# A transformer block in float32: the first tile's normalization ahead of the second tile's statistics, and the first batch's VectorE and GpSimd work in another order

## The chip, the cores and the metric

The kernel runs on one core of one Trainium2 chip. The metric is the device time of one execution in microseconds (us), lower is better. The profile shows one such execution. The engines are TensorE (PE, with its weight loads as PEld), VectorE (DVE), ScalarE (ACT), GpSimd (POOL) and SyncE (SP, which here only issues DMAs).

## The reference, cut to what matters

The input x has 8 batches of 1024 rows of 256 values, in float32. Each batch is normalized, goes through linear attention with l2-normed q and k, and through a two-layer network, and both are added to x:

```python
xn = _layernorm(x, axis=-1)
# attention, 16 heads of 16
qkv = (xn @ qkv_w + qkv_b).reshape(b, n, 3, H, D)
q, k, v = ...
q = q / max(norm(q), EPS);  k = k / max(norm(k), EPS)
kv = einsum('bhnd,bhne->bhde', k, v)
attn = einsum('bhnd,bhde->bhne', q, kv)  # then (b, n, c)
attn = attn @ proj_w + proj_b
# network, 256 -> 1024 -> 256
ffn = relu(xn @ W1 + b1) @ W2 + b2
return x + attn + ffn
```

## The kernel before, in words

A batch is 8 tiles of 128 rows (`NT`), two halves of four tiles (`HT`). The network's first layer, the projection to q and k (from batch 1 on), the product of k and xn and the second layer are computed by Strassen's scheme in Winograd's form: seven block products in place of eight, with sums of blocks formed ahead of the products (`sums_of_x`, `sums_of_h`, `sums_of_w2`, `g_sums`, on GpSimd) and sums of results formed from PSUM (`add`, on VectorE).

The order of all work is written out by hand: each engine executes its instructions in the order in which the program issues them. Buffers in PSUM come from a pool of seven banks (`bank`); an eighth tile takes the bank that the program's order freed first, and waits for its last reader.

*Head.* x of batch 0 is loaded in small pieces, the first two of one tile each. For tiles 0 and 1, `norm_stats` forms mean and variance (VectorE) and the root (ScalarE), `norm_scale` the reciprocal, `norm_apply` xn (VectorE, L276), and `turn_tile` transposes xn on TensorE (tpx, L899) and copies it out of PSUM on ScalarE (L900). `project(0)` then runs q and k of all eight tiles (pq, L331), with the normalization of tiles 2 to 7 in between, adds the bias on VectorE (L337), squares on ScalarE (L341) and sums the squares (L342).

*First layer, `hidden(b)`.* Twelve steps work on four blocks i: `first(i)` runs the products pha, phc and phd, with u1 copied by ScalarE and u2 and u3 formed by VectorE; `fifth(i)` runs phe; `last(i)` finishes three of the products; the relus (L650) are ScalarE's. The steps are, by number: 0 first(0), 1 fifth(0), 2 first(1), 3 last(0), 4 fifth(1), 5 first(2), 6 last(1), 7 fifth(2), 8 first(3), 9 last(2), 10 fifth(3), 11 last(3). After a step come `sums_of_x` of the next batch (steps 10 and 11), `sums_of_h` (0 after step 3, 1 after step 6, 2 and 3 after step 11), and the small steps that a table names: `first_steps` for batch 0, `later_steps` for the others.

*Small steps of batch 0.* `invert` turns the sums of squares into inverse norms: a maximum (L360, VectorE), a root (L361, ScalarE), a reciprocal (L362, VectorE). `scale` multiplies them into k and q (L474). `shift` adds one to a half of xn on ScalarE (L503), and `mix_g` multiplies k with xn (gp, L510) into gT. `fold_bias_of_v` folds the bias of v into its weights: a product of_rows (L493, TensorE), a (L495) and the sum onto the weights (L498), both VectorE. `mix_kv` (kvp, L604, then kvm on VectorE) reads these weights and gT; `mix_m` (mp, L621) reads kvm. The next batch's statistics and xn (L250 to L276) are formed; `turn_x`, called four times, transposes xn in blocks on VectorE (L298), each time followed by four DMAs on SP's queue (L300) that bring the parts to their partitions. After the twelve steps q of batch 0 is transposed on TensorE (tpq, L286), and `project_by_sums(1)` begins with pqa (L406).

After that, `second(b)` runs the second layer and the last product with q, and stores; all further batches follow the same pattern with `later_steps`.

Of the kernel before, what the change touches and what calls it, by code (L numbers as in the profile page):

```python
# [10 lines left out]
AF = mybir.ActivationFunctionType  # L11
# [5 lines left out]
def kernel(  # L17
# [34 lines left out]
    nc = tc.nc  # L52
# [5 lines left out]
    NT = N // P  # L58
    HT = NT // 2
# [5 lines left out]
    R = P // S  # L65
# [3 lines left out]
    L2_EPS = 1e-12  # L69
# [15 lines left out]
    def squares_v(v, b, n, j):  # L85


        return v[b].rearrange("(n s r t) (j c) -> n j s r t c", n=2, s=S, r=R, j=R)[n, j]

    def bank(shape, name):  # L90

        return psum.tile(shape, F32, tag="bank", name=name)
# [15 lines left out]
    def load_squares(b, halves=(0, 1)):  # L108
        xqs[b] = one.tile([P, 2, R, HT, CJ], F32, tag="xq", name=f"xq_{b}")
        for n in halves:  # L110
            for j in range(R):
                nc.sync.dma_start(out=xqs[b][ts(j, S), n], in_=squares_v(x, b, n, j))
# [124 lines left out]
    def s3_of_x(b):  # L237

        a11, a12, a21, a22 = halves(xnTs[b])
        nc.gpsimd.tensor_tensor(a21, a11, a21, ALU.subtract)  # L240
# [3 lines left out]
    def norm_stats(b, tiles):  # L244

        xt, n = xs[b], len(tiles)
        st = work.tile([P, NT, 6], F32, tag="st", name=f"st_{b}_{tiles[0]}")[:, :n, :]
        mv = small.tile([P, NT, 2], F32, tag="mv", name=f"mv_{b}_{tiles[0]}")[:, :n, :]
        for i, t in enumerate(tiles):
            nc.vector.bn_stats(st[:, i, :], xt[:, t, :])  # L250
        for i in range(n):
            nc.vector.bn_aggr(mv[:, i, :], st[:, i, :])
        rstd = small.tile([P, NT], F32, tag="rstd", name=f"rstd_{b}_{tiles[0]}")[:, :n]
        nc.scalar.activation(rstd, mv[:, :, 1], AF.Sqrt, bias=eps_sb)
        for i, t in enumerate(tiles):
            stats[b, t] = i, mv, rstd

    def norm_scale(b, tiles, on_act):
        i, mv, rstd = stats[b, tiles[0]]
        nc.vector.reciprocal(rstd, rstd)  # L260
        if on_act:
            nmr = small.tile([P, NT], F32, tag="nmr", name=f"nmr_{b}_{i}")[:, : len(tiles)]
            nc.vector.scalar_tensor_tensor(nmr, mv[:, :, 0], -1.0, rstd, ALU.mult, ALU.mult)  # L263
            for t in tiles:
                stats[b, t] += (nmr,)

    def norm_apply(b, tiles):
        for t in tiles:
            xt, xn = xs[b][:, t, :], xns[b][:, t, :]
            i, mv, rstd, *nmr = stats.pop((b, t))  # L270
            if nmr:
                nc.scalar.activation(  # L272
                    xn, xt, AF.Identity, bias=nmr[0][:, i : i + 1], scale=rstd[:, i : i + 1]
                )
            else:
                nc.vector.tensor_scalar(  # L276
                    xn, xt, mv[:, i, 0:1], rstd[:, i : i + 1], ALU.subtract, ALU.mult
                )
# [28 lines left out]
    def turn_x(b):  # L307

        if b not in xnTs:
            xnTs[b] = big.tile([P, KC, NP, P, 2], F32, tag="xnT", name=f"xnT_{b}")  # L310
            turns["x", b] = turn(xnTs[b], xns[b], f"x_{b}")
        next(turns["x", b])

    def project(b, within={}, held_to=0, with_norms=True):


        xnT = xnTs[b]
        if b not in qks:
            qks[b] = one.tile([P, NT, 2 * C], F32, tag="qk", name=f"qk_{b}")
        qk = qks[b]  # L320
        late, held = [], []
        for h in range(2):
            ss = small.tile([P, HT, 2 * H], F32, tag="ssk" if h else "ssq", name=f"ss_{b}_{h}", bufs=1)
            all_ss[b, h] = ss
            for s in range(2):
                norms_of[b, h, s] = ss[:, :, ts(s, H)]
            for i in range(HT):
                t = h * HT + i
                pq = bank([P, 512], f"pq_{b}_{t}")
                for kc in range(KC):  # L330
                    nc.tensor.matmul(  # L331
                        pq, xnT[:, kc, t // 2, :, t % 2], wqkv_sb[:, kc, 0 : 2 * C],
                        start=(kc == 0), stop=(kc == KC - 1), skip_group_check=True,
                    )
                    if kc == 0:
                        within.get(t, lambda: None)()
                nc.vector.tensor_tensor(qk[:, t, :], pq, qkvb_sb[:, 0 : 2 * C], ALU.add)  # L337

                def square(t=t, ss=ss, i=i):
                    sq = work.tile([P, 2 * C], F32, tag="yt", name=f"sq_{b}_{t}")  # L340
                    nc.scalar.activation(sq, qk[:, t, :], AF.Square)  # L341
                    return lambda: nc.vector.tensor_reduce(  # L342
                        ss[:, i, :], sq.rearrange("p (g d) -> p g d", d=D), AX.X, ALU.add
                    )

                held.append(square)
                while held and t >= held_to:
                    late.append(held.pop(0)())
                    while len(late) > 1:
                        late.pop(0)()  # L350
                if i == HT - 1 and with_norms:
                    late.append(lambda h=h, ss=ss: norms(b, h, ss))
        while late:
            late.pop(0)()

    norms_of, all_ss = {}, {}

    def invert(ss):

        nc.vector.tensor_scalar_max(ss, ss, L2_EPS * L2_EPS)  # L360
        nc.scalar.activation(ss, ss, AF.Sqrt)  # L361
        nc.vector.reciprocal(ss, ss)  # L362

    def norms(b, h, ss):
        invert(ss)
        scale(nc.gpsimd, b, h, 1)

    wt = const.tile([P, 3, C], F32, tag="wt", name="wt")
    dbias = const.tile([P, C], F32, tag="dbias", name="dbias")
# [101 lines left out]
    def scale(eng, b, h, s):  # L471

        part = qks[b][:, ts(h, HT), ts(s, C)].rearrange("p t (g d) -> p t g d", d=D)
        eng.tensor_tensor(  # L474
            part, part,
            norms_of[b, h, s].unsqueeze(3).to_broadcast([P, HT, H, D]), ALU.mult,
        )

    def scale_q(b, h):
        scale(nc.gpsimd if b == 0 else nc.vector, b, h, 0)  # L480

    def turn_q(b):

# [5 lines left out]
    def fold_bias_of_v():  # L489

        wv = wqkv_sb[:, :, of_v]
        of_rows = bank([P, C], "of_rows")
        nc.tensor.matmul(of_rows, mean, wv[:, 0, :], start=True, stop=True)  # L493
        a = one.tile([P, C], F32, tag="ksum", name="a")
        nc.vector.scalar_tensor_tensor(  # L495
            a, qkvb_sb[:, of_v], 1.0 / P, of_rows, ALU.mult, ALU.subtract
        )
        nc.vector.tensor_tensor(wv, wv, a.unsqueeze(1).to_broadcast([P, KC, C]), ALU.add)  # L498

    def shift(b):  # L500

        part = xns[b][:, :, 0:P]
        nc.scalar.activation(part, part, AF.Identity, bias=ones)  # L503

    def mix_g(b):
        qk, xn = qks[b], xns[b]
        gp = ps_mix.tile([P, KC, C], F32, tag="mix", name=f"gp_{b}")
        for f in range(KC):
            for t in range(NT):
                nc.tensor.matmul(  # L510
                    gp[:, f, :], xn[:, t, ts(f, P)], qk[:, t, C : 2 * C],
                    start=(t == 0), stop=(t == NT - 1),
                )
        gT = one.tile([P, KC, C], F32, tag="gT", name=f"gT_{b}")
        nc.scalar.copy(gT, gp)
        mixes[b] = gT
# [205 lines left out]

    def first_steps(b):

        lo, hi = range(HT), range(HT, NT)
        return {
            0: [lambda: load_squares(b)] + [lambda h=h: norms(b, h, all_ss[b, h]) for h in range(2)],
            1: [
                lambda: norm_stats(b + 1, lo), lambda: scale_q(b, 0), lambda: scale_q(b, 1),
            ],  # L730
            2: [lambda: shift(b), lambda: norm_stats(b + 1, hi), lambda: norm_scale(b + 1, lo, True)],
            4: [
                lambda: norm_scale(b + 1, hi, False), lambda: norm_apply(b + 1, lo),
                lambda: norm_apply(b + 1, hi), fold_bias_of_v, lambda: mix_g(b),
            ] + [lambda: turn_x(b + 1)] * R,
            5: [lambda: shift(b + 1), sums_of_w2, lambda: g_sums(b + 1, 0)],
            6: [lambda: mix_kv(b)],
            10: [lambda: mix_m(b)],
            11: [lambda: load(b + 2)],
        }  # L740

# [159 lines left out]

    for t in range(2):
        norm_stats(0, (t,))
    for t in range(2):
        norm_scale(0, (t,), False)
        norm_apply(0, (t,))
        turn_tile(t)
# [16 lines left out]
    def tiles_4_to_7():  # L924
# [5 lines left out]
        sums_of_x(0, 0)  # L930
        sums_of_x(0, 1)

    project(0, {1: tiles_2_3, 3: tiles_4_to_7}, 3, False)
    s3_of_x(0)
    sums_of_wqk()
    load(1)
# [70 lines left out]
```

## Time and profile before

| what | value |
|---|---|
| three runs, median (lowest to highest) | 617.99 us (617.8 to 619.47) |
| the profiled execution's own time | 617.92 us |
| its span in the profile | 616.1 us |
| TensorE busy | 606.6 us (98%) |
| VectorE, GpSimd, ScalarE busy | 417.3, 423.6, 211.5 us |
| pqa, the first product of batch 1's projection, starts at | 59.43 us |
| poa of batch 0's second layer starts at | 71.5 us |

Times in the timeline count from the start of the span. A row has start, duration, engine, line, operation, output<-inputs and count; in square brackets stands how long the engine was idle before it, and what ended that. A row of the waits reads: engine, tile and line that waited, what it waited for, then total, times and longest in us. Rows of the timeline are merged where the same line follows itself on an engine; the row's duration is then that of the whole stretch.

### The profile page before, as it was taken

How to read it: one execution, taken by the hardware profiler on the slowest of the kernel's cores; microseconds unless marked ns; L12 is line 12 of the kernel's file. 1: busy time of each engine (PE TensorE's matmuls, PEld its weight loads, DVE VectorE, ACT ScalarE, POOL GpSimd, SP SyncE). 2: the span in 40 equal slices, each digit the busy share in tenths (PEclk: the TensorE clock that was granted, in tenths of full speed). 3: DMA queues.
4: the chain of work that ended last, by engine and by line, in shares of the span. 5: the costliest groups of instructions: out<-in, count | busy, mean ns of one | idle time of the engine just before them, and what ended most of it. 6: DMA issues, size and time to landing. Idle time of an engine off the chain costs nothing.

```text
span 616.1 us, 6712 instructions
## 1 busy us (share of the span) xinstructions
PE 606.6 (98%) x2051; PEld 350.4 (57%) x2051; DVE 417.3 (68%) x741; ACT 211.5 (34%) x364; POOL 423.6 (69%) x347
## 2 busy tenths in 40 slices
PE   8999999999999999999999999999999999999996
PEld 5465755456644656447464484644755557644454
DVE  5896774777757776687665876567865777537823
ACT  5457223352334414243241532425224352103400
POOL 3788992599817996379944899339992599914701
PEclk9999999999999999999999999999999999999998
DMA  8615002670038400483005810158101640005302
GB/s 294 116 26 137 1 0 53 142 149 0 1 70 173 99 1 1 100 188 55 0 9 129 169 37 1 26 116 173 29 0 45 135 95 0 1 11 128 70 0 68
DMA packets 139940, 43.84 MB, mean 71 GB/s; under 512 B 135928, under 2 KB 136832, under 8 KB 139904
## 3 DMA queue, kind: packets, MB, share of 16 engines
q1 hardware_dynamic: 139184, 42.37, 31.2%
q10 hardware_dynamic: 720, 1.05, 0.5%
q8 instruction: 16, 0.26, 0.2%
q14 instruction: 20, 0.16, 0.1%
HBM read 20.32 MB, written 8.39 MB: 47 GB/s over the span
## 4 chain that ended last, share of the span: by engine, by line
PE 94%; DVE 3%; issue 1%; DMA 1%; ACT 1%; SPq 0%; DVEq 0%; ACTq 0%
PE poa L766 11%; PE poe L766 11%; PE pod L766 10%; PE phe L643 8%; PE phd L643 8%; PE pha L643 8%; PE poc L766 6%; PE phc L643 4%; PE pqa L406 4%; PE pqd L406 4%; PE pqe L406 4%; PE pq L331 2%; PE gpd L573 2%; PE gpe L573 2%; PE gpa L573 2%; PE pqc L406 2%
## 5 line engine op out<-in xcount | busy, mean ns | idle before, releaser
L803 POOL TENSOR_TENSOR xq<-xq,yt_o 128x512 f32<-128x512 f32 x30 | 38.0, 1265 | 127.3 <-DVE yt_o L798 124.3
L650 ACT ACTIVATE hT<-hT,b_sb 128x512 f32<-128x512 f32 x96 | 68.8, 722 | 60.6 <-DVE hT L655 55.9
L193 POOL TENSOR_TENSOR hS<-hT 128x512 f32<-128x512 f32 x31 | 46.3, 1492 | 34.4 <-ACT hT L650 34.4
L643 PE MATMUL pha<-xnT,w_sb 128*128 128x512 f32 x128 | 65.4, 592 | 0.0
L384 ACT ACTIVATE sq<-qk 128x512 f32<-128x512 f32 x56 | 33.8, 627 | 82.2 <-DVE qk L412 68.6
L766 PE MATMUL poa<-hT,w_sb 128*128 128x512 f32 x128 | 57.6, 592 | 0.0
L655 DVE TENSOR_TENSOR hT<-phe,u 128x512 f32<-128x512 f32 x64 | 43.7, 685 | 6.9 <-PE phe L643 5.3
L195 POOL TENSOR_TENSOR hS<-hT,hS 128x512 f32<-128x512 f32 x31 | 39.5, 1275 | 2.4
L798 DVE STREAM_TRANSPOSE yt_o<-y_o 128x512 f32<-128x512 f32 x30 | 33.3, 1109 | 11.7 <-ACT y_o L856 9.4
L194 POOL TENSOR_TENSOR hS<-hS,hT 128x512 f32<-128x512 f32 x31 | 39.5, 1274 | 2.4
L197 POOL TENSOR_TENSOR hT<-hT 128x512 f32<-128x512 f32 x31 | 40.0, 1289 | 0.0
L669 ACT COPY u<-pha 128x512 f32<-128x512 f32 x32 | 18.4, 575 | 56.4 <-PE pha L643 56.4
L766 PEld LDWEIGHTS poa<-hT,w_sb 128*128 128x128 f32 x128 | 23.8, 190 | 24.2 <-issue 23.9
L643 PEld LDWEIGHTS pha<-xnT,w_sb 128*128 128x128 f32 x128 | 23.8, 190 | 23.4 <-issue 22.2
L655 DVE TENSOR_TENSOR u<-phc,u 128x512 f32<-128x512 f32 x32 | 21.8, 682 | 20.8 <-ACT u L669 11.2
L643 PE MATMUL phc<-xS,w1t 128*128 128x512 f32 x64 | 32.8, 594 | 0.3 <-ACT hT L650 0.3
L650 ACT ACTIVATE hT<-pha,b_sb 128x512 f32<-128x512 f32 x32 | 21.8, 682 | 32.7 <-PE pha L643 32.7
L643 PE MATMUL phe<-xS,w_sb 128*128 128x512 f32 x64 | 32.7, 592 | 0.0
L643 PE MATMUL phe<-xS,w1t 128*128 128x512 f32 x64 | 32.7, 592 | 0.0
L643 PE MATMUL phd<-xnT,w_sb 128*128 128x512 f32 x64 | 32.7, 592 | 0.0
L643 PE MATMUL phd<-xnT,w1t 128*128 128x512 f32 x64 | 32.7, 592 | 0.0
L272 ACT ACTIVATE x<-x,nmr,rstd 128x256 f32<-128x256 f32 x58 | 29.6, 589 | 0.5 <-DVE nmr L263 0.4
(200 smaller groups left out, 1322.9 us busy)
## 6 DMA issues: line engine op xcount, KB each, us to landing
x<-in_L_attn_x_dram SPq DMA_DIRECT2D x15, 512.0 KB, 6.3
xq<-in_L_attn_x_dram SPq DMA_DIRECT2D x60, 128.0 KB, 3.6
out_dram<-xq SPq DMA_DIRECT2D x60, 128.0 KB, 2.9
xnT<-turn_x SPq DMA_DIRECT2D x112, 64.0 KB, 2.1
qT<-turn_q SPq DMA_DIRECT2D x112, 64.0 KB, 2.2
w_sb<-in_L_ffn_W_dram SPq DMA_DIRECT2D x2, 512.0 KB, 5.4
w_sb<-in_L_ffn_W_dram SPq DMA_DIRECT2D x8, 128.0 KB, 3.0
x<-in_L_attn_x_dram SPq DMA_DIRECT2D x3, 256.0 KB, 5.6
```

The lines of the kernel that those rows point to most:

```text
L193: eng.tensor_tensor(s1, a21, a22, ALU.add)
L194: eng.tensor_tensor(s2, s1, a11, ALU.subtract)
L195: eng.tensor_tensor(s4, a12, s2, ALU.subtract)
L197: eng.tensor_tensor(a21, a11, a21, ALU.subtract)
L384: nc.scalar.activation(sq, part_of_qk(b, n, g, m), AF.Square)
L406: nc.tensor.matmul(dst[:, w, :], a[:, g, :, w], rhs, start=start and w == 0, stop=stop, skip_group_check=True,)
L573: nc.tensor.matmul(dst, l[:, t, :], r[:, t, :], start=start and t == 0, stop=stop and t == HT - 1, skip_group_check=True,)
L643: nc.tensor.matmul(dst, lhsT, rhs, start=start, stop=stop, skip_group_check=True)
L650: nc.scalar.activation(block(i, n, m), src, AF.Relu, bias=b1_sb[:, fc : fc + 1])
L655: nc.vector.tensor_tensor(dst, p, q, ALU.add)
L766: nc.tensor.matmul(dst, l, r, start=start and n == 0, stop=stop and n == len(lhs) - 1, skip_group_check=True,)
L803: nc.gpsimd.tensor_tensor(xh, xh, yt.rearrange("p u w r c -> p (u w) r c"), ALU.add)
```

## The change

At the head, tile 0's reciprocal, xn and transposition are issued ahead of tile 1's statistics, where both tiles' statistics came first.

For batch 0, the inverse norms of k and of q are formed apart (`norms_of_first(1)` in step 0 for k, `norms_of_first(0)` in step 4 for q), and both of q's scales move from GpSimd in step 1 to VectorE in steps 9 and 10. Batch 1's statistics move from steps 1 and 2 to step 4, in one piece of eight tiles; all eight xn of batch 1 are formed by ScalarE in step 4, where ScalarE had four and VectorE four. `mix_g` comes ahead of the fold's product of_rows; the fold's VectorE part moves to the end of step 6, and `mix_kv` from step 6 to step 8. The four calls of `turn_x` move from step 4 to steps 4, 5, 6 and 6; `shift(1)` goes from step 5 to 7 and `g_sums(1, 0)` from step 5 to 8.

```diff
-    def norms(b, h, ss):
-        invert(ss)
-        scale(nc.gpsimd, b, h, 1)
+    def norms_of_first(s):
+
+        parts = [norms_of[0, h, s] for h in range(2)]
+        for p in parts:
+            nc.vector.tensor_scalar_max(p, p, L2_EPS * L2_EPS)
+            nc.scalar.activation(p, p, AF.Sqrt)
+        for p in parts:
+            nc.vector.reciprocal(p, p)
...
     def scale_q(b, h):
-        scale(nc.gpsimd if b == 0 else nc.vector, b, h, 0)
+        scale(nc.vector, b, h, 0)
...
         nc.tensor.matmul(of_rows, mean, wv[:, 0, :], start=True, stop=True)
+        yield
         a = one.tile([P, C], F32, tag="ksum", name="a")
...
         nc.vector.tensor_tensor(wv, wv, a.unsqueeze(1).to_broadcast([P, KC, C]), ALU.add)
+        yield
...
     def first_steps(b):
 
-        lo, hi = range(HT), range(HT, NT)
+        nxt, fold = range(NT), fold_bias_of_v()
         return {
-            0: [lambda: load_squares(b)] + [lambda h=h: norms(b, h, all_ss[b, h]) for h in range(2)],
-            1: [
-                lambda: norm_stats(b + 1, lo), lambda: scale_q(b, 0), lambda: scale_q(b, 1),
+            0: [lambda: load_squares(b), lambda: norms_of_first(1)]
+            + [lambda h=h: scale(nc.gpsimd, b, h, 1) for h in range(2)],
+            2: [lambda: shift(b)],
+            4: [
+                lambda: norm_stats(b + 1, nxt), lambda: norm_scale(b + 1, nxt, True),
+                lambda: norm_apply(b + 1, nxt), lambda: mix_g(b), lambda: next(fold),
+                lambda: norms_of_first(0), lambda: turn_x(b + 1),
             ],
-            2: [lambda: shift(b), lambda: norm_stats(b + 1, hi), lambda: norm_scale(b + 1, lo, True)],
-            4: [
-                lambda: norm_scale(b + 1, hi, False), lambda: norm_apply(b + 1, lo),
-                lambda: norm_apply(b + 1, hi), fold_bias_of_v, lambda: mix_g(b),
-            ] + [lambda: turn_x(b + 1)] * R,
-            5: [lambda: shift(b + 1), sums_of_w2, lambda: g_sums(b + 1, 0)],
-            6: [lambda: mix_kv(b)],
-            10: [lambda: mix_m(b)],
+            5: [sums_of_w2, lambda: turn_x(b + 1)],
+            6: [lambda: turn_x(b + 1), lambda: turn_x(b + 1), lambda: next(fold)],
+            7: [lambda: shift(b + 1)],
+            8: [lambda: mix_kv(b), lambda: g_sums(b + 1, 0)],
+            9: [lambda: scale_q(b, 0)],
+            10: [lambda: mix_m(b), lambda: scale_q(b, 1)],
             11: [lambda: load(b + 2)],
         }
...
     for t in range(2):
         norm_stats(0, (t,))
-    for t in range(2):
         norm_scale(0, (t,), False)
         norm_apply(0, (t,))
         turn_tile(t)
```

`project` no longer calls `norms` and loses the parameter `with_norms`, which batch 0, its only caller, had set to false.

More of the change, by code (lines that the diff above doesn't have):

```diff
@@ L312, in turn_x, with project @@
         next(turns["x", b])
-    def project(b, within={}, held_to=0, with_norms=True):
+    def project(b, within={}, held_to=0):
         xnT = xnTs[b]
@@ L323, in project @@
             ss = small.tile([P, HT, 2 * H], F32, tag="ssk" if h else "ssq", name=f"ss_{b}_{h}", bufs=1)
-            all_ss[b, h] = ss
             for s in range(2):
@@ L350, in project @@
                         late.pop(0)()
-                if i == HT - 1 and with_norms:
-                    late.append(lambda h=h, ss=ss: norms(b, h, ss))
         while late:
             late.pop(0)()
-    norms_of, all_ss = {}, {}
+    norms_of = {}
     def invert(ss):
@@ L931, in tiles_4_to_7 @@
         sums_of_x(0, 1)
-    project(0, {1: tiles_2_3, 3: tiles_4_to_7}, 3, False)
+    project(0, {1: tiles_2_3, 3: tiles_4_to_7}, 3)
     s3_of_x(0)
```

## The prediction

> **What bounds the kernel now.** First I read the busy times and the shares of the chain of waits, then who makes TensorE wait, then the timeline of the first 60 us, where all of the change lies.
>
> ```profile
> PE 606.6 (98%) x2051; PEld 350.4 (57%) x2051; DVE 417.3 (68%) x741; ACT 211.5 (34%) x364; POOL 423.6 (69%) x347
> ...
> PE 94%; DVE 3%; issue 1%; DMA 1%; ACT 1%; SPq 0%; DVEq 0%; ACTq 0%
> ```
>
> The chain that ends last is TensorE's own queue. Only idle of TensorE can be won, and idle put into it is lost for good: by the table of stretches it is busy 74.00 of 74.00 us from 60 to 134, so nothing later takes up a delay. TensorE's waits (line, releaser: total, times, longest) are few:
>
> ```profile
> PE of_rows L493 <- DVE u L655: 1.1, 1, 1.1
> PE tpx L899 <- DVE x L276: 1.1, 1, 1.1
> ...
> PE phc L643 <- ACT hT L650: 0.3, 1, 0.3
> ```
>
> By starts of matmuls, which show a loss better than modelled ends: phe of block 1 starts at 31.15 and takes 0.86, of_rows starts at 33.30, not 32.01: 1.29 lost. phc of block 3 starts at 48.99, not 48.51, and the next 0.10 late: 0.58. Together 1.87 us, and 1.07 ahead of the first tpx. More than 2.9 us is not to be had. The timeline of the spots that decide (start, duration, engine, line):
>
> ```profile
> 4.14 0.30 ACT L254 ACTIVATE rstd<-mv,eps_sb 128x1 f32<-128x1 f32 x1 [1.91 <-DVE mv L252]
> 4.91 0.43 DVE L250 BATCH_NORM_STATS2 st<-x 128x6 f32<-128x256 f32 x1 [0.80 <-DMA x<-in_L_attn_x_dram]
> ...
> 6.11 0.96 PE L899 MATMUL tpx<-ident,x 128*128 128x128 f32 x4 [1.07 <-DVE x L276]
> ...
> 6.58 0.91 ACT L900 COPY xnT<-tpx 128x256 f32<-128x256 f32 x2 [0.70 <-PE tpx L899]
> ...
> 11.60 1.27 POOL L189 TENSOR_TENSOR w1t<-w_sb,w1t 128x512 f32<-128x512 f32 x1
> ...
> 12.11 0.78 DVE L263 SCALAR_TENSOR_TENSOR nmr<-mv,rstd 128x2 f32<-128x2 f32 x1
> ...
> 42.54 1.31 POOL L189 TENSOR_TENSOR w2t<-w_sb 128x512 f32<-128x512 f32 x1
> ...
> 43.09 1.31 DVE L498 TENSOR_TENSOR wqkv_sb<-wqkv_sb,a 128x512 f32<-128x512 f32 x1
> ...
> 44.33 2.48 DVE L298 STREAM_TRANSPOSE turn_x<-x 128x512 f32<-128x512 f32 x4
> ...
> 45.05 10.53 SPq L300 DMA_DIRECT2D xnT<-turn_x  x16
> ```
>
> Tile 0's root is there at 4.44, but VectorE, in order, waits for tile 1's data. Two VectorE operations with both inputs in SBUF, nmr and the fold (L498), stretch under a running GpSimd operation.
>
> **The Trainium skill.** "SBUF — State Buffer", Who interferes with whom: a VectorE instruction with two SBUF inputs, or in a two-port mode, and a GpSimd instruction that reads SBUF exclude each other; the first holds the port for its whole length, and ScalarE never waits. The trace agrees: nmr takes 0.16 alone and 0.78 above, ending 0.02 after GpSimd's; the fold ends 0.55 after GpSimd's (an alike sum alone, L197: 0.68); ScalarE's xn take 0.585 to 0.602 throughout. "TensorE: Matmul & The Clock Gate", What's actually happening: an idle window of about 3.4 us lowers the clock. At the head idle grows from 1.07 to some 1.4 us, and the trace grants 1.00 there, so I charge nothing.
>
> **The change part by part**, in the clock of the profile before.
>
> *First tile.* Reciprocal 4.48, xn 4.65 to 5.06, tpx_0 at 5.11 instead of 6.11. But pq_0 stands behind tpx_1 on TensorE, and ScalarE now has copy_0 (0.47 after tpx_0: 5.58 to 6.03) ahead of tile 1's root. That root starts at about 5.98, before at 5.59; reciprocal 6.32, xn 6.52 to 6.92, tpx_1 6.96 (6.62), pq_0 7.41 (7.07). From pq_0 to 22.7 TensorE runs without a gap, so **+0.34** passes on. Were the root not held it would be +0.03; a gain is excluded, since tile 1's statistics start only behind xn_0.
>
> *Norms and scales.* k's maxima 26.20 to 26.95, roots to 27.40, two reciprocals of 64 columns (0.55 each, between 0.14 for 1 column and 0.95 for 128), GpSimd scales k 27.8 to 31.7. Statistics no longer stand ahead of block 1: relu, u1 (30.09), x's shift (31.14) and VectorE's five sums end by 33.4. gp, now ahead of of_rows, needs k at 31.7 and the shift, and starts at 32.01 without a wait. GpSimd loses the two q scales (3.86). **−1.29**, and −0.58 if the phc wait goes too.
>
> *From there TensorE wants*, at 6.91 for gp, 0.54 for of_rows and 0.86 each: block 2's phe at 44.62, block 3's phc at 46.34, kvp at 48.06, and pqa at 57.56.
>
> *What VectorE can give.* Eight statistics 33.32 (0.33 each) and aggregates end 36.7, root 37.02, nmr issued 37.29. GpSimd's sums of block 0, earlier by the same 4 us as their relu, then have their last operation at 36.96 to 38.28: nmr ends 38.3. Eight xn on ScalarE (4.04 for eight at 93.5) end 42.4; then gT's copy and the two roots of q end 43.3. VectorE's reciprocals of q wait behind these roots, from 41 to 43.1, and everything behind them: reciprocals to 44.1, transpose 0 44.1 to 44.8, u2 of block 2 44.7 to 45.4. The four VectorE xn (4.92) are gone, but this wait returns half of it.
> The banks come free in program order, and of_rows now keeps its own until the end of step 6. So block 2's phe gets u2's bank: 45.42, not 44.62, 0.80 late. Then VectorE does u3 45.5, transpose 1 46.1, sums of block 1 at 46.7 and 47.3 (phc of block 3 takes the first one's bank: 47.45, 0.3 late), transposes 2 and 3 to 49.2, and only then the fold, issued 49.6. TensorE wants kvp at 49.17 by then. GpSimd's sums of block 1 have their first operation end at 49.5 and the second start at 49.6, which I cannot order against the fold: fold ends 50.15 if first, 51.4 if behind it. **kvp waits 1.0 or 2.3.**
> Behind the fold stand block 2's last sum, its relu, batch 1's shift (1.15, now ahead of u1 on ScalarE), u1, u2 (53.1 or 54.35), u3 and kvm (55.0 or 56.2); mp wants kvm 0.5 earlier. Then two sums and scale_q, 1.22 each by VectorE's row at L474, two SBUF inputs; one at 56.1 runs free, one at 57.3 falls under GpSimd's xS sums and waits for 58.3. The block's next sum frees phe of block 3 0.35 or 1.3 late; the second scale ends at 59.8 or 62.0, 0.1 late for tpq's second half. pqa starts at **60.7 or 62.95, before 59.43**.
>
> *The moved DMAs.* The 16 of the transposes go out in four groups behind four transposes. At 0.66 each SP needs 10.5 us; the first goes at 44.9, groups 1 to 3 are ready before SP gets there, so they land about 0.2 earlier than now, under 57.25. load(2) stands behind them and has a batch to land. sums_of_w2 (5.4) starts as block 0's sums end and fills GpSimd's pause till block 1's relu; g_sums of batch 1 (2 x 1.3), moved behind them, run till 56.1 or 56.6, hidden until its k is projected; beyond 57.25 they would push the xS sums. GpSimd's xS sums start there as before and are wanted only after pqa. The fold, costing TensorE nothing now (kvp at 45.9, fold done 44.4), loses its cover, which is the mechanism of my forecast.
>
> *Sum.* 60.7 − 59.43 + 0.34 = +1.6, or 62.95 − 59.43 + 0.34 = +3.9. The profiled execution took 617.92 with 616.1 of span and 1.8 around it; the median is 0.07 higher. So 619.5 or 621.8. Neither order of the fold and GpSimd's sum is likelier, and the later clashes can fall between; I take the middle, **620.6**.
>
> **Rivals.** *No new wait* (18%): VectorE gets nmr in ahead of GpSimd's last sum (1.0 earlier) and slips the fold between two of its operations, so the fold is done near 49 as kvp is wanted. The old waits go, 617.92 − 1.87 + 0.34 = 616.4. It decides at this one place: kvp and what hangs on it may come 1.5 late in all (1.87 − 0.34) before the change costs time. For it speaks that VectorE loses 4.92 of blocked xn; against it that q's roots still stand behind eight xn and a copy. *The head gains too* (7%): if pq_0 isn't held by tile 1, 1.0 more is won, 615.1 to 615.5; against it TensorE's order. *A wash* (7%): of_rows' wait is repaid by the phe and kvp waits alone, with q's scale hidden: −1.87 + 0.80 + 0.3 + 1.0 + 0.34 = +0.6, 618.5. That the change does nothing is excluded, the queues are in written order.
>
> **How the numbers follow.** My forecast has 68%. A measurement of this kernel can tell about 0.3%, 1.85 us: the line lies at 619.8, inside my two values, so of the 68 I put 50 above and 18 within. The wash is within; of no new wait 9 are within, 9 faster by a little more; the head's 7 split 6 to 1. Faster 0.15, same 0.35, slower 0.50. The range reaches from 616.0, just short of the head's case, to 622.2, the later order and 0.4 more, a third of one further GpSimd turn of 1.3.
>
> **What would show it.** Right: tpx at 5.1 but pq at 7.4; no wait at of_rows; nmr near 1 us long; VectorE idle some 2 us ahead of q's reciprocals; TensorE waiting at phe for u2, at kvp for L498 for 1 to 2.3, then at mp, phe and tpq. Wrong: kvp without a wait, pqa before 59.4, or pq at 7.1 or earlier.

## The result

The changed kernel takes 621.09 us (median of ten runs, 619.53 to 621.87), the kernel before 618.11 us beside it (617.8 to 620.68). The ratio is 1.0036, with a 95% interval of 1.0022 to 1.0051: slower by about a third of a per cent. The profiled execution of the changed kernel took 619.53 us with a span of 617.7 us, 1.6 us more than the profiled one of before in both. So the profile, of a run at the low end, shows 1.6 us of the 3.0 between the medians. The experiments look for the cause of both parts.

The page of the changed kernel, busy times and shares of the chain that ended last, and then TensorE's waits (tile, line, releaser: total us, times, longest):

```profile
PE 606.9 (98%) x2051; PEld 350.3 (57%) x2051; DVE 416.5 (67%) x742; ACT 212.7 (34%) x369; POOL 421.0 (68%) x345
...
PE 92%; DVE 4%; ACT 1%; issue 1%; DMA 0%; DVEq 0%; ACTq 0%
```

```profile
PE tpx L905 <- DVE x L276: 1.5, 2, 1.3
...
PE kvp L608 <- DVE wqkv_sb L501: 0.9, 1, 0.9
PE phe L647 <- DVE u L659: 0.7, 1, 0.7
PE phe L647 <- DVE hT L659: 0.3, 1, 0.3
...
PE mp L625 <- PE phe L647: 0.2, 1, 0.2
```

Busy times say nothing here; they moved by less than 3 us on every engine. The waits tell the case: of_rows and phc are gone from the list, and kvp, two phe and mp have come. The timeline shows what stands behind each:

```profile
1.36 3.68 PE L898 MATMUL warm<-ident 128*128 128x128 f32 x16 [1.36 <-POOL ident masks.py:199]
...
5.21 0.52 PE L905 MATMUL tpx<-ident,x 128*128 128x128 f32 x2 [0.18 <-DVE x L276]
...
5.77 0.38 ACT L906 COPY xnT<-tpx 128x256 f32<-128x256 f32 x1 [1.26 <-PE tpx L905]
6.04 0.29 ACT L254 ACTIVATE rstd<-mv,eps_sb 128x1 f32<-128x1 f32 x1
...
7.03 0.44 PE L905 MATMUL tpx<-ident,x 128*128 128x128 f32 x2 [1.30 <-DVE x L276]
7.31 2.75 PE L330 MATMUL pq<-wqkv_sb,xnT 128*128 128x512 f32 x6
...
37.53 1.10 DVE L263 SCALAR_TENSOR_TENSOR nmr<-mv,rstd 128x8 f32<-128x8 f32 x1
...
38.66 4.04 ACT L272 ACTIVATE x<-x,nmr,rstd 128x256 f32<-128x256 f32 x8 [1.41 <-DVE nmr L263]
...
43.36 0.96 DVE L368 RECIPROCAL ss<-ss 128x64 f32<-128x64 f32 x2 [3.45 <-ACT ss L366]
...
44.24 0.66 DVE L298 STREAM_TRANSPOSE turn_x<-x 128x512 f32<-128x512 f32 x1
...
45.53 1.13 PE L647 MATMUL phe<-xS,w1t 128*128 128x512 f32 x2 [0.70 <-DVE u L659]
...
49.61 0.69 DVE L501 TENSOR_TENSOR wqkv_sb<-wqkv_sb,a 128x512 f32<-128x512 f32 x1
49.66 1.77 POOL L194 TENSOR_TENSOR hS<-hS,hT 128x512 f32<-128x512 f32 x1
50.45 1.13 PE L608 MATMUL kvp<-gT,wqkv_sb 128*128 128x128 f32 x8 [0.95 <-DVE wqkv_sb L501]
...
59.31 1.91 PE L286 MATMUL tpq<-ident,qk 128*128 128x128 f32 x16
61.05 1.03 PE L408 MATMUL pqa<-wqkv_sb,xnT 128*128 128x256 f32 x4
```

The first tpx starts 0.9 us earlier, and pq, the first work that matters, 0.28 later: ScalarE's root of tile 1 (6.04) runs behind the copy of tile 0 (5.77). VectorE sits idle for 3.45 us ahead of q's reciprocals. The fold got the port that it shares with GpSimd by 0.05 us; GpSimd's sum, whose record starts at 49.66, took 1.77 instead of 1.27. pqa starts at 61.05, before at 59.43: +1.62. Of that 0.22 comes back by the second batch's poa (147.32 against 145.92), the last matmul ends 1.4 later, and the span 1.6.

### The profile page after: what moved, and what is told of

It is laid out like the page before. It is cut to its first block, busy times and chain, and to the rows that moved or that the text cites. A ratio compares the mean times of both kernels' runs of the same rounds, so it can differ in the third digit from the quotient of the medians.

```text
span 617.7 us, 6716 instructions
## 1 busy us (share of the span) xinstructions
PE 606.9 (98%) x2051; PEld 350.3 (57%) x2051; DVE 416.5 (67%) x742; ACT 212.7 (34%) x369; POOL 421.0 (68%) x345
## 4 chain that ended last, share of the span: by engine, by line
PE 92%; DVE 4%; ACT 1%; issue 1%; DMA 0%; DVEq 0%; ACTq 0%
PE poa L772 11%; PE poe L772 11%; PE pod L772 10%; PE phe L647 8%; PE pha L647 8%; PE phd L647 8%; PE poc L772 6%; PE pqa L408 4%; PE pqd L408 4%; PE pqe L408 4%; PE phc L647 4%; PE pq L330 2%; PE gpe L577 2%; PE gpd L577 2%; PE gpa L577 2%; PE pqc L408 2%
## 5 line engine op out<-in xcount | busy, mean ns | idle before, releaser
L197 POOL TENSOR_TENSOR hT<-hT 128x512 f32<-128x512 f32 x31 | 39.9, 1287 | 0.0
L272 ACT ACTIVATE x<-x,nmr,rstd 128x256 f32<-128x256 f32 x62 | 31.5, 590 | 2.0 <-DVE nmr L263 1.8
```

Of the source, the lines that this page charges most:

```text
L197: eng.tensor_tensor(a21, a11, a21, ALU.subtract)
```

## The experiments

A measure that the head does not touch is the distance from the first product of the first layer (pha) to pqa: the head drops out, and the change's first-batch part is all inside. The column "full clock" is the moment at which the trace's first record of a full granted clock of TensorE begins. Each ratio is to the runs of the kernel before that were taken beside it, whose medians lie between 618.10 and 619.16; medians of different rows are therefore only roughly comparable. Starts in us:

| kernel | full clock | pha | pqa | pha to pqa | median us | ratio to before (95%) |
|---|---|---|---|---|---|---|
| before | 5.05 | 22.55 | 59.43 | 36.88 | 618.11 | |
| changed | 5.43 | 22.73 | 61.05 | 38.32 | 621.09 | 1.0036 (1.0022 to 1.0051) |
| after_again | 13.06 | 25.91 | 64.24 | 38.33 | 620.72 | 1.0026 (1.0015 to 1.0038) |
| fold_first | 10.03 | 24.99 | 63.29 | 38.30 | 620.49 | 1.0021 (1.0009 to 1.0033) |
| fold_behind | 10.07 | 25.04 | 63.36 | 38.32 | 620.56 | 1.0028 (1.0016 to 1.0039) |
| head_only | 10.87 | 24.97 | 61.84 | 36.87 | 619.69 | 1.0011 (0.9999 to 1.0023) |
| before_warm | 7.03 | 22.72 | 59.58 | 36.86 | 618.02 | 0.9988 (0.9979 to 0.9998) |
| after_warm | 6.98 | 23.83 | 62.13 | 38.30 | 620.41 | 1.0023 (1.0015 to 1.0031) |
| fold_in_4_warm | 7.06 | 23.93 | 61.71 | 37.78 | 619.93 | 1.0014 (1.0004 to 1.0024) |
| q_roots_early_warm | 7.24 | 23.79 | 60.62 | 36.83 | 618.28 | 0.9994 (0.9982 to 1.0006) |
| fold_behind2_warm | 6.06 | 23.83 | 64.00 | 40.17 | 622.62 | 1.0067 (1.0054 to 1.0079) |
| best_warm | 5.49 | 23.09 | 59.12 | 36.03 | 617.01 | 0.9975 (0.9966 to 0.9984) |
| best_pq0_warm | 6.17 | 22.70 | 58.74 | 36.04 | 617.07 | 0.9972 (0.9963 to 0.9982) |
| best_q_on_gpsimd | 10.14 | 24.94 | 59.91 | 34.97 | 616.05 | 0.9956 (0.9942 to 0.9969) |

pha to pqa repeats within 0.03 us in five profiles with the changed order (changed, after_again, fold_first, fold_behind, after_warm). pha itself moves by 3 us between two executions of the changed kernel.

**What the scatter is.** My first thought was that the two orders of the fold and GpSimd's sum, which I could not tell apart in the prediction, made the runs scatter from 619.5 to 621.9. Three kernels were meant to show that: the changed one again, one that holds GpSimd up, one that holds VectorE up.

```diff
# fold_first: GpSimd, between the first and second sum of block 1
+eng.memset(padt[:, 0:1], 0.0)
+eng.memset(padt[:, 1:2], 0.0)
# fold_behind: VectorE, ahead of the sum onto the weights
+for i in range(4):
+    nc.vector.memset(pad[:, i : i + 1], 0.0)
```

> The changed kernel unaltered. Theory: its runs fall into two groups, near 619.5 us where the fold onto the weights (VectorE) gets in ahead of GpSimd's second sum of block 1, and near 621.7 us where it comes behind; the profile shows one of the two, with kvp starting at 50.4 or at about 51.7 and pqa at 61.0 or about 63.3. Rival: the scatter of 619.5 to 621.9 is disturbance from outside the program; then the time does not go with the order seen in the profile.

> As the changed kernel, but GpSimd does two small memsets (about 0.1 us each) between its first and second sum of block 1, so that the fold on VectorE comes first. Theory: always the short order, 619.5 us within 0.5, kvp at 50.4, fold 0.69 us long, ratio to the kernel before about 1.0025. Rival (scatter from outside): median about 621, as wide as the changed kernel's.

> As the changed kernel, but four small memsets (0.06 us each) on VectorE ahead of the fold, which then asks after GpSimd's second sum has begun. Theory: always the long order, fold ends about 51.5, kvp at about 51.6, 621.5 to 622 us, ratio about 1.006. Rival: the 0.25 us of memsets is all that is added, 0.25 us to the changed kernel's time.

All three have the fold first and the same pha to pqa, and all three scatter as the changed kernel does, from 619.0 to 622.7. Neither padded kernel did what its edit says. In fold_behind the four memsets put the fold off by only some 0.04 us, and it still came first, at 51.92 against 51.96. In fold_first GpSimd's two memsets ran in the gap that lies between its sums anyway (0.07 us, 0.08 in the changed kernel). The theory fell all the same: the profiled executions of the three took 622.19, 621.65 and 621.73 us, the times that it gave to the other order, with the fold first in each. What differs is the head. In after_again's timeline:

```profile
5.24 0.69 PE L905 MATMUL tpx<-ident,x 128*128 128x128 f32 x2 [0.21 <-DVE x L276]
7.24 0.69 PE L905 MATMUL tpx<-ident,x 128*128 128x128 f32 x2 [1.30 <-DVE x L276]
7.72 5.33 PE L330 MATMUL pq<-wqkv_sb,xnT 128*128 128x512 f32 x6
```

The same six records of pq took 2.75 us in the changed kernel's first profile and 5.33 here: half pace. The profile's table of stretches prints a granted clock of 1.00 at the head of both, but that is no measurement: it counts time ahead of the trace's first clock record as 1.00. The timeline contradicts it, for the 16 warm-up transpositions take 3.68 us where 16 transpositions of the same shape in tpq take 1.91. The records themselves begin at 5.43 us in the first profile and at 13.06 in the second. In each profile the matmuls are at half pace until that moment (a pq record starts 0.85 behind the one before it) and at full pace after it (0.43).

The Trainium skill, "TensorE: Matmul & The Clock Gate", What's actually happening, describes it: the array starts at half its clock, comes up after a busy window of about 3.4 us, and the windows do not start with the kernel. The trace agrees: the long stretches of full clock in its records are multiples of 3.413 us to within rounding (607.57 us, 178 of them, in the kernel before), and they begin at another moment in each execution. The 16 warm-up matmuls are busy for 3.67 us and then leave a hole of 1.07 us (0.18 and 1.30 in the changed kernel), so where the window falls decides whether pq runs at full pace. I tested that by filling the hole, in the kernel before and in the changed one:

```diff
# before_warm
-    WARM = 16
+    WARM = 20
# after_warm, in turn_tile
         nc.scalar.copy(xnTs[0][:, :, t // 2, :, t % 2], tp)
+        if t == 0:
+            warm2 = bank([P, HT, P], "warm2")
+            for i in range(5):
+                nc.tensor.transpose(warm2[:, i % HT, :], ident, ident)
```

> The kernel before with 20 instead of 16 warm-up transpositions (0.23 us each), which fill TensorE's idle ahead of the first tpx. Theory: the three groups of times of the kernel before (617.7, 619.2, 620.4) are the head's matmuls at half pace for 0, some or 6 of them (0.43 more each), which depends on when TensorE's clock comes up; without the hole it comes up earlier, so most runs lie near 617.7 and the median is 0.5 to 1.5 us below that of before. Rival: the groups come from elsewhere (DMA); then they stay.

> The changed kernel with five transpositions of the identity (0.23 us each) between tile 0's and tile 1's tpx, where TensorE idles 1.3 us. Theory: its runs gather near 619.3, 1.6 us above the filled kernel before: the queues' part of the change is +1.6 us, the rest of the measured difference is the clock at the head. Rival: the queues cost the whole measured 2 to 3 us, then it stays near 620.7.

For the kernel before, 20 of 22 runs then lie between 617.7 and 618.2; of the 67 runs of the unfilled one beside it, 39 lie below 618.3 and the rest reach 620.7. The theory held; only the gain of the median (0.5 to 1.5 expected, 0.08 measured) did not come, as most runs of before were good ones there. The clock records say the same: full clock begins at 7.24 us or earlier in all six profiles with four or five extra transpositions, and at 5.05, 5.43 or 10.0 to 13.1 in the six without. In all, 99 of 191 runs of before lie below 618.4. Of the 76 runs of the changed kernel and the two padded ones, which share its head, 23 lie below 619.8. head_only, the first part of the change alone, has one run of 14 near the lowest, at 618.08:

```diff
 for t in range(2):
     norm_stats(0, (t,))
-for t in range(2):
     norm_scale(0, (t,), False)
```

> The kernel before with the first part of the change alone: tile 0's xn and transposition ahead of tile 1's statistics. Theory: tpx of tile 0 about 1.0 us earlier, but pq of tile 0 and all that follows 0.2 to 0.35 us later, because tile 1's root waits behind tile 0's copy on ScalarE; time +0.2 to +0.35 us. Rival: the earlier tpx is a gain, 0.5 to 1.0 us shorter.

Its pha to pqa is 36.87, as before, so the head's part does not reach into the first layer. Its interval holds 1 and cannot tell +0.2 from nothing; what it excludes is the rival's gain. Its profile has half pace too (pq from 7.73, full clock at 10.87).

after_warm did not gather near 619.3 as expected. It has two groups, 7 runs from 619.3 to 619.6 and 15 from 620.2 to 620.7, and its median of 620.41 is near the rival's value. But the queues do not cost more in it: its pha to pqa is 38.30. Its profile, one of the second group, shows a further race, between VectorE and GpSimd for their port. First the changed kernel, then after_warm:

```profile
11.74 0.16 DVE L263 SCALAR_TENSOR_TENSOR nmr<-mv,rstd 128x2 f32<-128x2 f32 x1
...
11.85 1.27 POOL L189 TENSOR_TENSOR w1t<-w_sb,w1t 128x512 f32<-128x512 f32 x1
```

```profile
11.78 1.27 POOL L189 TENSOR_TENSOR w1t<-w_sb,w1t 128x512 f32<-128x512 f32 x1
11.80 1.26 DVE L263 SCALAR_TENSOR_TENSOR nmr<-mv,rstd 128x2 f32<-128x2 f32 x1
...
14.98 0.93 PE L905 MATMUL tpx<-ident,x 128*128 128x128 f32 x4 [0.29 <-ACT x L272]
```

nmr of tiles 4 and 5 comes 0.11 us ahead of GpSimd's second sum in the one and 0.02 behind it in the other. That puts the xn of these tiles and of tiles 6 and 7 off by 1.1, and pha comes 1.10 later (23.83 against 22.73) with pq at full pace in both. The three further profiles with this head lost the race too (nmr 1.08 to 1.20 long, pha 23.79 to 23.93). So one part of the scatter is shown as the clock and one as this race; how often each strikes in an unprofiled run I did not measure.

**What in the queues costs 1.44 us.** Two theories were left from the prediction: q's norms, behind eight xn on ScalarE, set the pace of VectorE; or the late place of the fold does. Each was undone alone, with the filled head:

```diff
# fold_in_4_warm
-lambda: norms_of_first(0), lambda: turn_x(b + 1),
+lambda: next(fold), lambda: norms_of_first(0), lambda: turn_x(b + 1),
...
-6: [lambda: turn_x(b + 1), lambda: turn_x(b + 1), lambda: next(fold)],
+6: [lambda: turn_x(b + 1), lambda: turn_x(b + 1)],
# q_roots_early_warm: norms_of_first keeps the reciprocals only
-0: [lambda: load_squares(b), lambda: norms_of_first(1)]
+0: [lambda: load_squares(b), lambda: roots_of_first(1), lambda: roots_of_first(0), lambda: norms_of_first(1)]
```

> The changed kernel with the filled head, and VectorE's two fold operations moved from the end of step 6 to step 4, ahead of q's norms, where VectorE waits for ScalarE anyway. Theory: kvp's wait (0.95) goes, of_rows' bank comes free early so that block 2's phe no longer waits for u2, and all behind the fold comes about 1.1 us earlier: pqa 1.3 to 1.7 us earlier against the changed kernel with the same head, about 617.8. Rival (q's norms set the pace, the fold only follows): under 0.5 us.

> The changed kernel with the filled head, and the maxima and roots of q's norms moved from step 4 to step 0, behind those of k; the reciprocals stay in step 4. Theory: VectorE's wait of 3.45 us ahead of them goes, the first transposition starts when batch 1's xn are done, about 1.5 us earlier (42.7, not 44.2), phe's wait for u2 goes and kvp's shrinks to nothing: 1.3 to 1.6 us less than the changed kernel with the same head. Rival (the fold's place sets it): under 0.5 us.

Measured from pha to pqa against after_warm, moving the fold gained 0.52, about its rival's size, not 1.3 to 1.7. Moving q's maxima and roots gained 1.47, as much as the change had lost. VectorE in the two kernels, the fold moved and then the roots moved:

```profile
42.83 1.36 DVE L365 TENSOR_SCALAR ss<-ss 128x64 f32<-128x64 f32 x2
44.55 0.96 DVE L368 RECIPROCAL ss<-ss 128x64 f32<-128x64 f32 x2 [0.36 <-ACT ss L366]
45.43 0.66 DVE L298 STREAM_TRANSPOSE turn_x<-x 128x512 f32<-128x512 f32 x1
```

```profile
39.23 0.95 DVE L365 RECIPROCAL ss<-ss 128x64 f32<-128x64 f32 x2
43.41 0.72 DVE L298 STREAM_TRANSPOSE turn_x<-x 128x512 f32<-128x512 f32 x1 [3.24 <-ACT x L272]
```

From pha the first transposition is 21.50 away with the fold moved, 21.51 in the changed kernel, and 19.62 with the roots moved. Moving the fold empties kvp's wait and phe's for u2, but mp then waits 1.16 us for kvm, which still follows the late transpositions. With the roots moved two details of the expectation failed: VectorE's pause did not go, it still waits 3.24 us, now for the xn themselves, and kvp still waits 0.72 for the fold. What went is the time between the last xn and the first transposition, in which ScalarE's copy and roots and VectorE's reciprocals had stood. The pause that is left is free for the fold.

**The price of the other order.** Two one-column reciprocals put the fold off by 0.3 us:

```diff
+for _ in range(2):
+    nc.vector.reciprocal(root, root)
 nc.vector.tensor_tensor(wv, wv, a.unsqueeze(1).to_broadcast([P, KC, C]), ALU.add)
```

> The changed kernel with the filled head and two one-column reciprocals (about 0.15 us each) on VectorE ahead of the fold's sum, so that it asks when GpSimd's second sum of block 1 has begun. Theory (the prediction's later order): the fold ends at that sum's end, about 1.2 us later, kvp waits 2.1 to 2.3, and with the later clashes pqa comes 1.2 to 2.3 us later than with the fold first. Rival: VectorE gets the port between anyway, then 0.3 us.

```profile
50.76 1.26 POOL L194 TENSOR_TENSOR hS<-hS,hT 128x512 f32<-128x512 f32 x1
50.86 1.71 DVE L503 TENSOR_TENSOR wqkv_sb<-wqkv_sb,a 128x512 f32<-128x512 f32 x1
...
52.72 1.13 PE L610 MATMUL kvp<-gT,wqkv_sb 128*128 128x128 f32 x8 [2.11 <-DVE wqkv_sb L503]
```

Now GpSimd is first by 0.1, the fold takes 1.71 instead of 0.69, kvp waits 2.11 instead of 0.95, and pqa comes 1.87 later than with the fold first. But the order of the two is not all that differs. Behind kvp's wait the trace grants half the clock for one stretch of 3.41 us (start and end, length, busy time of PE, PEld, DVE, ACT and POOL, then the granted clock, DMA share and GB/s):

```profile
50.44:53.85 3.41, 1.30 (x10) 1.16 (x10) 2.70 (x5) 0.64 (x2) 3.25 (x4) 1.00 0.42 97
53.85:57.26 3.41, 3.41 (x5) 1.35 (x5) 1.69 (x4) 2.27 (x4) 3.21 (x3) 0.50 0.42 97
```

kvp starts 1.17 later than in after_warm, the matmuls at the end of that stretch 2.87 later, and pqa 1.87 later, because mp and the last phe then have no wait of their own left. So the 1.17 at kvp is the order's by itself; how the further 0.70 at pqa divides between later clashes and the clock is open.

**A version that beats both.** q's maxima and roots in step 0, q's reciprocals and the whole fold in step 4, batch 1's shift behind u1 of block 3 on ScalarE. best_warm takes the head of the kernel before with 20 warm-ups; best_pq0_warm issues pq of tile 0 ahead of tile 1; best_q_on_gpsimd adds to that q's first half on GpSimd in its pause:

```diff
+    lambda: norms_of_first(0), lambda: next(fold), lambda: turn_x(b + 1),
...
-7: [lambda: shift(b + 1)],
-8: [lambda: mix_kv(b), lambda: g_sums(b + 1, 0)],
+8: [lambda: shift(b + 1), lambda: mix_kv(b), lambda: g_sums(b + 1, 0)],
# best_pq0_warm: tile_1() issues tile 1's normalization and transposition
-project(0, {1: tiles_2_3, 3: tiles_4_to_7}, 3)
+project(0, {0: tile_1, 1: tiles_2_3, 3: tiles_4_to_7}, 3)
# best_q_on_gpsimd
-5: [sums_of_w2, lambda: turn_x(b + 1)],
+5: [sums_of_w2, lambda: scale(nc.gpsimd, b, 0, 0), lambda: turn_x(b + 1)],
-9: [lambda: scale_q(b, 0)],
-10: [lambda: mix_m(b), lambda: scale_q(b, 1)],
+9: [lambda: scale_q(b, 1)],
+10: [lambda: mix_m(b)],
```

> The changed kernel with the head of the kernel before (both statistics first) and 20 warm-up transpositions; q's maxima and roots in step 0; q's reciprocals and then the whole fold in step 4, where VectorE waits for batch 1's xn; batch 1's shift in step 8, behind u1 of block 3 on ScalarE. Theory: no wait of TensorE over 0.2 us is left from the first product of the first layer (pha) to pqa, which is then 35.1 to 35.4 us (36.88 before, 38.32 changed): 1.5 to 1.8 us less than the kernel before, about 616.3, ratio 0.997. Rival: the waits turn up elsewhere (mp for kvm, tpq for q's scale), then no better than the kernel before.

> As the version with all of these, but with tile 0's xn first at the head and its first projection product (pq) issued ahead of tile 1's transposition, two extra transpositions of the identity behind tpx of tile 0, and 16 at the start. Theory: what kept the early tpx from paying was that pq stood behind tile 1; now pq starts near 6.2 us instead of 7.0, and 0.5 to 0.9 us are won on top, about 615.6. Rival: tiles 2 and 3 are then late and take it back, or the clock comes up later: 616.3 or more.

> As the version with pq of tile 0 ahead of tile 1, but the first half of q is scaled on GpSimd in step 5, in its 3.1 us pause behind the sums of the second layer's weights (1.93 us by its row), and the second half by VectorE in step 9; step 10 has none. Theory: tpq's wait for q's scale (0.85) goes, pqa is 35.2 us behind the first product of the first layer, time 0.8 us less than that version. Rival: GpSimd's sums of block 1 start later and push its xS sums, which pqd then waits for; no gain.

best_warm missed its 35.1 to 35.4 (36.03): tpq waits 0.85 for q's second scale, the kind of shift that its rival named. It is still faster than the kernel before. best_pq0_warm starts pq at 6.43 and yet gains nothing in the median over best_warm, so its rival's size came true; which of the rival's two reasons holds is not shown. best_q_on_gpsimd reaches 34.97, as its theory had it, and behind the start of the warm-ups TensorE waits for nothing over 0.3 us:

```profile
PE warm L900 <- POOL ident masks.py:199: 1.4, 1, 1.4
PE tpo L827 <- DVE y_o L886: 0.3, 1, 0.3
PE tpx L907 <- ACT x L272: 0.3, 1, 0.3
```

At 616.05 us it is faster than the kernel before (0.9956, 0.9942 to 0.9969), though its profile, of the slowest of its five runs, has pq's first four matmuls at half pace (full clock at 10.14).

## Why the prediction was right, point by point

The direction came out, and the mechanism of the queues did, step by step. That the number (620.6 against 621.09) is close is in part luck: the queues cost 1.6 us, the lower of my two values. The midpoint's extra 1.1 stood for a later order that no profile of the changed kernel shows, and it happens to lie near the 1.5 that the head's clock and the nmr race, which I had not priced, can add. (The 0.07 by which the median lies above the profiled execution was named in the sum and not added; it is below the noise.)

*First tile, +0.34.* The mechanism is shown: copy ahead of root, tpx of tile 1 at 7.03. The size was too large: pq follows that tpx by 0.28 and its six records run without the small break that before had (2.59 against 2.69 to the next tpx), so pha is 0.18 later, some 0.07 of which is x landing later in this execution.

*Waits removed, −1.87.* Right: gp starts at 32.17, and of_rows and phc are gone from the list of waits. By starts of matmuls phc of block 3 is 0.27 late, the 0.3 that the prediction gives for its bank.

*VectorE behind q's roots.* Right, and q_roots_early_warm shows it decisive: moving the maxima and roots returns 1.47, the whole net loss. With 0.18 added for the head, nmr was to end at 38.5 (38.63), the reciprocals to start at 43.3 (43.36), phe at 45.60 (45.53), kvp at 50.4 with the fold first (50.45), and pqa at 60.9 (61.05). The idle time ahead of the reciprocals was put at 2 us and is 3.45, since it begins at 39.9 and not at 41; its end, which counts, is right. tpq, put at 0.1 late, does not wait. What the Trainium skill, "SBUF — State Buffer", Who interferes with whom, says of the first holder agrees with both orders: behind the fold GpSimd's sum takes 1.77 and not 1.27, behind that sum the fold takes 1.71 and not 0.69. The claim that nothing later takes up a delay is 0.22 off: that much of 1.62 is back by the second batch's poa.

*The fold's two orders.* I called them equally likely. In all five profiles of the changed order the fold was first, by 0.04 to 0.06 us. So the step "I take the middle" failed: the queues alone give the lower value, 619.5, and that is what the profiled execution took (619.53). The later order was priced at 2.25 more; fold_behind2_warm measured 1.87, of which 0.70 came with a stretch of half clock that the price did not have, so it does not confirm the later clashes.

*The clock, "I charge nothing".* This is the term that was missing. I compared the hole with a whole idle window, and I read "the trace grants 1.00 there" off a table that prints 1.00 where the trace has no record; the first record of that profile begins at 5.05, just ahead of the first tpx, and its warm-ups ran at half pace. The question was whether the busy window ahead of pq was complete, and one profile cannot show a lottery. Half pace costs 2.58 us on six records, the nmr race 1.1 at pha. Together they can account for the median of the changed kernel, some 1.5 us above its lowest runs; the shares are not measured. The runs of the kernel before scatter too, about half of them above 618.4. That the longer hole makes it likelier is suggested by 23 of 76 runs against 99 of 191, not isolated.

*The fold, "which is the mechanism of my forecast".* The fold's lost cover is where TensorE waits longest, but moving it alone returned 0.52 of 1.44. The place that decides is upstream, the roots with what stands around them. The prediction had both in its chain and put the weight on the wrong one.

*Rivals.* No new wait is excluded by kvp's 0.95, the wash by the waits of mp and of block 3's phe (tpq did not wait, as the wash had it), the head's gain by pq at 7.31.

## What to carry to other kernels

Before moving small work to a roomier engine, ask what its small results stand behind there: q's two roots of 0.2 us, issued behind eight xn, put VectorE's first transposition off by 1.9 us (21.51 against 19.62 from pha) and cost TensorE 1.47. A wait that you can see on the bound engine (kvp on the fold) may not be the one to undo; trace it to the engine that fell idle first. Where gains are a few us, compare distances inside the timeline between two landmarks, and fill idle at the head ahead of timing anything.

## What the hardware showed unexpectedly

The moment at which TensorE's clock comes up varies between executions of one kernel: 5.43 and 13.06 us in two of the changed kernel, in which six records of pq take 2.75 and 5.33 us. A printed clock of 1.00 at the head says nothing of it; the pace of the matmuls does. Four more warm-up transpositions (0.9 us in a hole of 1.07) brought 20 of 22 runs to within 0.5 us. In the middle of a kernel a wait shorter than the idle window of 3.4 us that the prediction went by was enough to lose it: in fold_behind2_warm 2.11 us, with TensorE busy for 1.30 of the last 3.41 us, was followed by 3.41 us at half clock. That is one execution. And the order of VectorE and GpSimd at their common SBUF port is decided by hundredths of a us and costs a whole operation: 0.11 ahead or 0.02 behind made nmr 0.16 or 1.26 us long, and pha 1.1 us later.
